# Two edge groups per step with a transposed second layer, and a gather that is partly replaced by column copies, in a graph-network kernel on one Trainium2 core

## The chip, the cores and the metric

The kernel runs on one core of one Trainium2 chip. The metric is the device time of the whole program in microseconds (us); lower is better. The core has five engines that run their own instruction streams and meet at semaphores: PE (matrix products, with weight loads shown as PEld), ACT (activations, and one queue that issues transfers), DVE (element-wise work), POOL (here it issues the indirect gathers), and SP (it issues transfers). On each engine instructions start in program order.

## The reference, cut to what matters

There are N = 12,500 nodes with 64 features and E = 200,000 edges, sorted by `dst`.

```python
nodes = x[edges].reshape(E, 128)               # x[src] beside x[dst]
ssp = lambda v: softplus(v) - log(2)
gates = ssp(edge_state @ We1 + be1) @ We2 + be2
gates = gates * (1 - sigmoid(5.0 * (dist - 3.5)))
h = ssp(nodes @ Wn1 + bn1) @ Wn2 + bn2         # Wn1 128x128, Wn2 128x64
sums = zeros_like(x).at[dst].add(h * gates)
new = x + ssp(sums @ Ws1 + bs1) @ Ws2 + bs2
out = layernorm(x + new)
```

All of it is float32.

## The kernel before

**Tiling.** Edges are cut into 391 groups of 512 (four slots of 128 edges each, called k = 0 to 3). A group's edge features `eT` stand feature-major, two halves of 256 edges stacked on 128 partitions. Its `x[src]` rows are gathered edge-major into a tile `xg` (128 edges on the partitions, 4 slots of 64 features); `x[dst]` is not gathered: `dst` is sorted, so a window of W = 42 nodes covers a half group, a precomputed `table` holds x @ Wn1's lower half plus bias for each node, and a one-hot matrix of 42 columns (line 293, DVE) selects from that window. The one-hot columns lie behind the 64 features in `xg`.

**One step** (loop of lines 632 to 678, one group ahead in layer 1, `i+1`, and one behind in layer 2, `i`):

- SP issues the loads of group `i+5` (lines 273 to 288) and 7 single-row transfers (256 B each, lines 249 to 263); POOL issues up to four gathers of group `i+14` (line 231).
- PE transposes the four slots of `i+1` (lines 304 and 307), ACT copies the result `xT` out of PSUM (line 314), and ACT issues 9 single-row transfers in three portions of three, after this copy, after the exponential and after the logarithm. The rows so fetched by SP and ACT fill some slots (47 of them) which POOL then does not gather. Row addresses come from eight register loads at a time (line 245).
- PE runs the bias and edge products of layer 1 (lines 319 and 324), the bias of layer 2 (354), the scatter product of group `i-2` (383) and, when `xT` is there, the node product of layer 1 (330).
- ACT takes the exponential (341) and the logarithm (344) of 768 columns; DVE forms the softplus `s` (349).
- PE runs layer 2 of group `i`: two products for the gates (361) and four for the hidden part (366). Here `s` is the stationary operand (a new weight load for each) and `We2` or `Wn2` moves 128 or 64 columns, so that the result `gh` is edge-major. DVE multiplies by the cutoff (375) and forms the message (379). The scatter product multiplies messages by the one-hot columns, and DVE adds the result to `sums` at a window whose place is read into registers (lines 391 and 400).

When enough groups are through, a block of nodes is finished in small parts placed into the following steps (`node_block`, lines 402 to 483). The order on each engine is written by hand (`tc.manual_schedule`); waits for buffers come from the tile pools: `xg` has AHEAD + BEHIND = 19 buffers, `z`, `gh` and `tx` in PSUM two each.

A float32 product is recorded as two matmul instructions with two weight loads; a transpose as one.

Of the kernel before, what the change touches and what calls it, by code (L numbers as in the profile page):

```python
# [69 lines left out]
PREPARE = 5  # L70
BEHIND = 5
CLOSE = 12

# [5 lines left out]
READY = (5, 7)  # L79
LANDED = 4  # L80
CUTOFF = 5.0
EPS = 1e-5
# [22 lines left out]
def slots_by_rows(NG):  # L105

    slots = []
    for queue in range(2):
        n = 0
        for g in range(READY[queue], NG - 2):  # L110
            if (g - READY[queue] - ROWS_FROM + 1) * ROWS[queue] >= (n + 1) * P:
                slots.append((queue, g, K - 1 - queue))
                n += 1
    return slots


# [7 lines left out]
def gnn_resnorm_kernel(ctx: ExitStack, tc: tile.TileContext, a: dict, out: bass.AP, E: int):  # L124
# [55 lines left out]
    eps = const.tile([P, 1], F32, name="eps")  # L180
    ones3 = const.tile([PIECES, HE], BF16, name="ones3")
    be3 = const.tile([PIECES, 2, D], BF16, name="be3")
    row3 = const.tile([PIECES, 2, K, D], BF16, name="row3")
    rs3 = const.tile([PIECES, K, D], BF16, name="rs3")
    wns = const.tile([DW, REST, 2, 2 * D], F32, name="wns")

    xgs, xrs, eTs = {}, {}, {}
    made = {}
# [32 lines left out]
    def gather(g):  # L221

        xg = loads.tile([P, K, P], F32, name="xg", bufs=AHEAD + BEHIND)
        xgs[g] = xg
        for k in range(K):
            if (g, k) in by_rows:
                continue
            if padding(g, k):
                nc.vector.memset(xg[:, k, :D], 0.0)
                continue  # L230
            note(("gather", g), nc.gpsimd.indirect_dma_start(  # L231
                out=xg[:, k, :D], out_offset=None, in_=x,
                in_offset=bass.IndirectOffsetOnAxis(ap=src_i[:, g, k : k + 1], axis=0)))
# [39 lines left out]
    def load(g):  # L273
        old = ("scatter", g - LOADS - 4)
        if g % 2 == 0:
# [3 lines left out]
            for j in range(n):  # L279
                eTs[g + j] = both[:, j]  # L280
            _, at = nc.values_load_multi_w_load_instructions(
                base_i[32:33, 2 * g : 2 * g + 4], engines=[SP], min_val=0, max_val=8 * D * (N - 1),
                skip_runtime_bounds_check_because="they were clamped to these bounds")
            bases[g], bases[g + 1] = at[:2], at[2:]
        for h in range(2):
            behind(note(("load", g), nc.sync.dma_start(
                wns[D:DW, g % REST, h, :].bitcast(U8),
                table_bytes[:, bass.ds(bases[g][h], 8 * D * W)].rearrange("o (w f) -> (o w) f", w=W))), old)

    xTs, zs, us, ss, ghs, hs, msgs, scs = ({} for _ in range(8))  # L290
# [26 lines left out]
    def layer1_bias(g, *needs):  # L317
        zs[g] = z_tile()
        first = nc.tensor.matmul(zs[g][:, 0, :HE], be3.rearrange("q h d -> q (h d)"), ones3, start=True, stop=False,  # L319
                                 skip_group_check=True)  # L320
        behind(first, *needs)

    def layer1_edge(g):
        nc.tensor.matmul(zs[g][:, 0, :HE], we1.rearrange("a h d -> a (h d)"), eTs[g], start=False, stop=True,  # L324
                         skip_group_check=True)

    def layer1_node(g):
        for h in range(2):
            zn = zs[g][:, h, HE * (1 - h) : HE * (2 - h)]
            nc.tensor.matmul(zn, wns[:, g % REST, h, :], xTs[g][:, h], start=True, stop=True,  # L330
                             skip_group_check=True)

# [5 lines left out]
    def exps(g, part=every):  # L338
        if part.start == 0:
            us[g] = work.tile([P, 3 * HE], F32, name="u")  # L340
        nc.scalar.activation(us[g][:, part], z_of(g)[:, part], AF.Exp)  # L341
# [4 lines left out]
    def softplus(g, part=every):  # L346
        if part.start == 0:
            ss[g] = work.tile([P, 3, 2, P], F32, name="s", bufs=3)
        nc.vector.scalar_tensor_tensor(ss[g].rearrange("p i t e -> p (i t e)")[:, part], us[g][:, part], BIG,  # L349
# [27 lines left out]
    def message(g):  # L377
        msgs[g] = work.tile([P, K, D], F32, name="msg", bufs=3)
        nc.vector.tensor_mul(msgs[g], ghs[g][:, 0], hs[g])  # L379
# [15 lines left out]
    def window(g):  # L395
        if g not in window_at:
            window_bases(g)
        for h in range(2):
            part = sums[h * D : (h + 1) * D, bass.ds(window_at[g][h], W)]
            nc.vector.tensor_add(part, part, scs[g][h * D : (h + 1) * D, h * W : (h + 1) * W])  # L400

    def node_block(first, n, pool):
# [87 lines left out]
    with tc.manual_schedule():  # L490
# [4 lines left out]
        with tc.tile_pool(name="prep", bufs=1) as prep:  # L495
# [11 lines left out]
            for i in range(3):  # L507
                load_x(i)
            nc.sync.dma_start(rows_i, a["rows"])
            dist = cut.rearrange("p g k -> p (g k)")  # L510
            nc.sync.dma_start(dist, a["dist_l"])
# [3 lines left out]
            for g in range(AHEAD):  # L515
# [13 lines left out]
            nc.scalar.dma_start(wns[:D].rearrange("f r h o -> f (r h) o"),  # L529
                                a["Wn1"][:D, :].rearrange("f (r o) -> f r o", r=1).to_broadcast([D, 2 * REST, 2 * D]))  # L530

            dst_f = dst_h.bitcast(F32)
# [45 lines left out]
            nc.scalar.dma_start(row_d.rearrange("(o q) f -> o q f", o=1), pieces)  # L578
            rows = prep.tile([PIECES, 4, D], BF16, name="rows")
            nc.scalar.dma_start(rows.rearrange("q i d -> q (i d)"), row_d)  # L580
            for i in range(3, PARTS):
# [4 lines left out]
            for i in range(PARTS):  # L586
# [10 lines left out]
                if i == 1:  # L597
                    nc.vector.tensor_copy(base_i[:1], base_b[:1])
                    nc.vector.tensor_scalar(base_i[32:33], base_b[32:33], float(8 * D), None, OP.mult)
                    nc.vector.tensor_scalar(rows_i, rows_i, float(4 * D), None, OP.mult)  # L600
                    for k in range(2):
                        nc.vector.tensor_copy(be3[:, k, :], rows[:, 0, :])
                    for k in range(K):
                        nc.vector.tensor_copy(row3[:, :, k, :], rows[:, 1:3, :])
# [9 lines left out]

        with tc.tile_pool(name="finish", bufs=1) as finish:
            blocks = list(zip(node_blocks(N), block_steps(N, NG)))
            last = NG - 1
            parts, begun, complete, rest = {}, None, 0, []

# [3 lines left out]

            def behind_by(i):
                close = last - CLOSE
                return [g for g in ([i - 2] if i <= close else []) + ([i - 1] if i >= close else []) if g >= 0]

            for g in range(LOADS - 1):
                load(g)
            for g in range(2):  # L630
                onehot(g)
            for i in range(-1, last - 1):
                now = parts.pop(i, [])
                early = [part for part in now if part.tensor]
                at(load, i + LOADS)
                read_rows(i, 0, ROWS[0])
                fetch(i, 0, ROWS[0])
                if i >= 0:
                    at(gather, i + AHEAD)
                transposes(i + 1, ("load", i + 1), ("gather", i + 1), ("onehot", i + 1))  # L640
                xcopy(i + 1)
                read_rows(i, 1, ROWS[1])
                fetch(i, 1, ROWS[1] - 6)
                layer1_bias(i + 1)
                at(layer2_bias, i)
                for n, g in enumerate(behind_by(i)):
                    scatter(g, zs[i + 1][:, 1, HE + 2 * n * W : HE + 2 * (n + 1) * W])
                layer1_edge(i + 1)
                layer1_node(i + 1)
                exps(i + 1)  # L650
                fetch(i, 1, 3)
                logs(i + 1)
                fetch(i, 1, 3)
                for g in behind_by(i):
                    window(g)
                at(layer2, i)
                for part in early:
                    part.tensor(tx_tile())
                at(hcut, i)
                at(message, i)  # L660
                softplus(i + 1)
                for part in early:
                    part.others()
                at(onehot, i + 3)
                for part in now:
                    if not part.tensor:
                        part.others()
                complete = i
                if blocks and complete >= blocks[0][1] - PREPARE and not begun:
                    begun = node_block(*blocks[0][0], finish)  # L670
                    begun.pop(0).others()
                if blocks and complete >= blocks[0][1]:
                    steps = next(steps for steps in BLOCK_STEPS if i + steps[-1] < last - 1)
# [3 lines left out]
                    blocks.pop(0)  # L677
                    begun = None
            assert len(blocks) == 1 and begun and not parts

# [44 lines left out]
    with tc.If(far > 0), tc.tile_pool(name="outside", bufs=1) as o:  # L725
# [7 lines left out]
        with tc.For_i(0, NG, 1) as g:  # L733
# [20 lines left out]
            for k in range(K):  # L754
# [3 lines left out]
            z = z_tile()  # L758
            nc.tensor.matmul(z[:, 1, :HE], be3.rearrange("q h d -> q (h d)"), ones3, start=True, stop=False,
                             skip_group_check=True)  # L760
# [39 lines left out]
def layouts(inputs):  # L800
# [22 lines left out]
    for queue, columns in enumerate(row_columns(NG)):  # L823
        chosen = [out["src_l"].reshape(P, NG, K)[:, g, k] for q, g, k in slots_by_rows(NG) if q == queue]
        v = padded(np.concatenate(chosen), P * columns, 0).reshape(-1, P, READ)
        rows.append(v.transpose(1, 0, 2).reshape(P, columns))
    out["rows"] = np.ascontiguousarray(np.concatenate(rows, axis=1))
    out["dst_l"] = lanes(dst, dst[-1])
    out["dist_l"] = lanes(dist, 1e6)
# [43 lines left out]
```

## Time and profile before

| what | value |
|---|---|
| median of 3 runs (lowest, highest) | 2687.81 us (2668.61, 2691.71) |
| the profiled execution: time, span | 2686.47 us, 2684.7 us |
| mean granted clock of PE | 0.815 |
| first and last `xT` copy start at | 143.3 us, 2660.5 us of the span |
| PE busy, weight loads busy | 2243.6 us (84%), 1754.9 us (65%) |
| DVE, ACT, POOL busy | 1052.4, 969.6, 1441.8 us (39%, 36%, 54%) |
| gathers by POOL | 1516, 951 ns each |
| single-row transfers issued by ACT, by SP | 3328, 2688 |

In the profile a line such as `L330 PE MATMUL z<-xT,wns ... x1564 | 574.1, 503 | 322.9 <-ACT xT L314 309.5` is read so: source line and engine, operation, written tile and read tiles with shapes, number of instructions, then busy us in total and mean ns of one, then how long the engine stood idle just before these and what ended most of that idle time. `ACTq`, `SPq` and `DVEq` are the sequencers' own instructions: transfers issued and registers loaded. Ends of matmuls are modelled by the profiler. The work between 143.3 and 2660.5 us is 390 steps of the loop, so one step takes 6.45 us on average.

### The profile page before, as it was taken

The page shows a single profiled execution, that of the slowest core. Times are in us where ns is not written, and L with a number is a line of the kernel's source. Part 1 is how long each engine was busy: PE and PEld are TensorE (multiplying, and loading weights), DVE is VectorE, ACT ScalarE, POOL GpSimd, SP SyncE. Part 2 cuts the span into 40 slices and gives each one's busy share as a digit, 9 for nine tenths or more (in the row PEclk, how much of TensorE's full clock was granted, in tenths as well). Part 3 has the DMA queues.
Part 4 walks back from the last instruction along what each step waited for, and adds up shares of the span by engine and source line. Part 5 has one row for each costly group of instructions (what it writes and reads, how often), then busy time and mean ns, then how long its engine had stood idle before and what let it go on. Part 6 is the DMA issues. An engine that isn't in the chain of part 4 may idle for free.

```text
span 2684.7 us, 47845 instructions
## 1 busy us (share of the span) xinstructions
PE 2243.6 (84%) x11373; PEld 1754.9 (65%) x11373; DVE 1052.4 (39%) x2767; ACT 969.6 (36%) x1318; POOL 1441.8 (54%) x1520
## 2 busy tenths in 40 slices
PE   2489888988888888888889788888888888888897
PEld 1467666766666666666667666666666667666676
DVE  1233333333334333344333443434433443444445
ACT  0133333333333333333333333333334333333344
POOL 7335555555555555555555555555555555555520
PEclk9987788788788778788777888778878887787878
DMA  6222222222222212222222222222222222222210
GB/s 159 82 64 52 48 51 49 48 49 48 49 52 50 49 47 51 51 52 47 52 46 50 51 49 53 53 50 53 51 50 50 50 58 48 54 52 50 52 44 25
DMA packets 150911, 143.53 MB, mean 53 GB/s; under 512 B 51887, under 2 KB 98395, under 8 KB 150626
## 3 DMA queue, kind: packets, MB, share of 16 engines
q1 hardware_dynamic: 94090, 88.26, 11.6%
q0 software_dynamic: 48512, 49.77, 9.5%
q10 hardware_dynamic: 8024, 2.37, 0.4%
q8 instruction: 97, 1.59, 0.2%
q14 instruction: 188, 1.54, 0.2%
HBM read 130.59 MB, written 9.63 MB: 52 GB/s over the span
## 4 chain that ended last, share of the span: by engine, by line
PE 64%; another core or an unknown queue 11%; ACTq 10%; ACT 7%; issue 5%; DVE 1%; DMA 0%; DVEq 0%; SPq 0%
PE z L330 16%; PE gh L366 12%; PE z L383 10%; ACTq L257 10%; PE gh L361 7%; PE tx L307 6%; ACT xT L314 6%; PE z L324 4%; PE gh L354 3%; PE z L319 2%; PE tx L419 1%; PE z L591 1%; ACTq L245 1%; PE tx L450 1%
## 5 line engine op out<-in xcount | busy, mean ns | idle before, releaser
L231 POOL DMA_INDIRECT xg<-in_x,src_i x1516 | 1441.6, 951 | 1144.8 <-PE z L383 353.1
L330 PE MATMUL z<-xT,wns 106*128 106x256 f32 x1564 | 574.1, 503 | 322.9 <-ACT xT L314 309.5
L330 PEld LDWEIGHTS z<-xT,wns 106*128 106x128 f32 x1564 | 361.3, 246 | 486.6 <-ACT xT L314 407.9
L341 ACT ACTIVATE u<-z 128x768 f32<-128x768 f32 x392 | 317.4, 810 | 830.4 <-issue 362.4
L366 PE MATMUL gh<-consts,s 128*128 128x64 f32 x3128 | 493.1, 313 | 0.0
L400 DVE TENSOR_TENSOR sums<-sums,z 64x42 f32 x778 | 153.0, 197 | 863.4 <-issue 626.8
L366 PEld LDWEIGHTS gh<-consts,s 128*128 128x128 f32 x3128 | 490.2, 238 | 0.1
L314 ACT COPY xT<-tx 106x512 f32<-106x512 f32 x391 | 228.9, 586 | 670.9 <-remote 231.5
L375 DVE TENSOR_TENSOR h<-gh,cut 128x256 f32<-128x256 f32 x391 | 166.1, 425 | 618.2 <-PE z L383 239.7
L344 ACT ACTIVATE u<-u,one 128x768 f32<-128x768 f32 x392 | 365.9, 934 | 69.7 <-issue 53.3
L349 DVE SCALAR_TENSOR_TENSOR s<-u,z 128x768 f32<-128x768 f32 x392 | 369.4, 943 | 11.1 <-ACT u L344 9.8
L361 PEld LDWEIGHTS gh<-consts,s 128*128 128x128 f32 x1564 | 304.0, 247 | 70.1 <-DVE s L349 32.8
L383 PEld LDWEIGHTS z<-xg,msg 128*128 128x128 f32 x1556 | 240.3, 221 | 152.8 <-issue 148.5
L361 PE MATMUL gh<-consts,s 128*128 128x128 f32 x1564 | 313.8, 335 | 1.8 <-DVE s L349 1.8
L383 PE MATMUL z<-xg,msg 128*128 128x84 f32 x1556 | 306.2, 327 | 0.9 <-DVE msg L379 0.2
L324 PE MATMUL z<-eT,consts 128*128 128x256 f32 x782 | 295.4, 465 | 0.0
L307 PE MATMUL tx<-consts,xg 128*106 128x128 f32 x1517 | 278.6, 312 | 6.4 <-DMA wns<-table 6.4
L307 PEld LDWEIGHTS tx<-consts,xg 128*106 128x106 f32 x1517 | 216.0, 169 | 10.6 <-issue 8.0
L379 DVE TENSOR_TENSOR msg<-gh,h 128x256 f32<-128x256 f32 x391 | 166.0, 425 | 13.4
L354 PE MATMUL gh<-row,ones 3*128 3x512 bf16 x391 | 170.0, 435 | 0.0
L324 PEld LDWEIGHTS z<-eT,consts 128*128 128x128 f32 x782 | 141.7, 226 | 1.2 <-issue 1.2
L293 DVE TENSOR_TENSOR xg<-consts,rel 128x168 f32<-128x168 f32 x391 | 129.9, 332 | 0.0
(93 smaller groups left out, 609.5 us busy)
## 6 DMA issues: line engine op xcount, KB each, us to landing
xr<-in_x ACTq DMA_DIRECT2D x3328, 0.2 KB
eT<-in_eT SPq DMA_DIRECT2D x195, 256.0 KB
xr<-in_x SPq DMA_DIRECT2D x2688, 0.2 KB
xg<-in_x,src_i POOLq DMA_INDIRECT x1516
wns<-table SPq DMA_DIRECT2D x782, 21.0 KB
table<-tb SPq DMA_DIRECT2D x14, 448.0 KB
sums<-in_xT SPq DMA_DIRECT2D x7, 455.0 KB
y<-in_x SPq DMA_DIRECT2D x24, 128.0 KB
```

The source lines that it names most:

```text
L231: note(("gather", g), nc.gpsimd.indirect_dma_start(out=xg[:, k, :D], out_offset=None, in_=x, in_offset=bass.IndirectOffsetOnAxis(ap=src_i[ ...
L257: ins = queues[queue].dma_start(row_tiles[n, "in"][r : r + 1, :D].bitcast(U8), x_bytes[:, bass.ds(row_at[queue].pop(0), 4 * D)])
L307: ins = nc.tensor.transpose(tx[:, k, :], xgs[g][:, k, :DW], ident)
L314: note(("xcopy", g), nc.scalar.copy(xT, xTs[g]))
L324: nc.tensor.matmul(zs[g][:, 0, :HE], we1.rearrange("a h d -> a (h d)"), eTs[g], start=False, stop=True, skip_group_check=True)
L330: nc.tensor.matmul(zn, wns[:, g % REST, h, :], xTs[g][:, h], start=True, stop=True, skip_group_check=True)
L341: nc.scalar.activation(us[g][:, part], z_of(g)[:, part], AF.Exp)
L344: nc.scalar.activation(us[g][:, part], us[g][:, part], AF.Ln, bias=one)
L349: nc.vector.scalar_tensor_tensor(ss[g].rearrange("p i t e -> p (i t e)")[:, part], us[g][:, part], BIG, z_of(g)[:, part], OP.min, OP.max)
L361: nc.tensor.matmul(v[:, 0, t], ss[g][:, 0, t, :], we2, start=False, stop=False, skip_group_check=True)
L366: nc.tensor.matmul(ghs[g][:, 1, 2 * t + h, :], ss[g][:, 1 + h, t, :], wn2, start=False, stop=h == 1 and t == 1, skip_group_check=True)
L383: ins = nc.tensor.matmul(sc, msgs[g][:, 2 * t : 2 * t + 2, :].rearrange("p h f -> p (h f)"), xgs[g][:, 2 * t : 2 * t + 2, D:DW], start=t = ...
```

## The change

Groups 0 to 371 are now worked in 186 pairs, one pair per step (`PAIRS = 186`); the last groups keep the old step. In a pair's step:

- Layer 1's bias and edge products run once for both groups with 512 moving columns (`pair_edge`); the node products stay one set per group. The exponential, logarithm and softplus are done in two parts: 1024 columns (edges of both groups and nodes of the first) and 512 columns (nodes of the second).
- Layer 2 is feature-major: `We2` and `Wn2` are stationary and `s` moves 512 columns. `pair_gates` is one product; `pair_hidden` is two, each with the 64 columns of `Wn2` as weights, writing partitions 0 to 63 and 64 to 127 of one bank. ACT adds the gates' bias while it copies them out of PSUM (`pair_bias`, 128x512), DVE adds the hidden part's bias and multiplies (`pair_products`, 128x512), PE transposes the product back to edge-major (`pair_turn`, four transposes of 128x128), and DVE applies the cutoff (`pair_weigh`, 128x512). Scatter and windows of a pair come a step later.
- The step's gathers, one-hots, loads and single-row transfers are those of two groups: 14 rows by SP, 18 by ACT in six portions of three. ACT's logarithm of the first part is followed at once by the second group's `xT` copy.
- x is loaded once, transposed and in two halves stacked on the partitions, into an SBUF tile `xh` of 6250 columns. From group 8 on DVE copies 16 columns of it a pair (two calls of `columns`, each eight register loads and eight copies of one 128x1 column at a register's place) into a tile of 128 columns, the `x[src]` of one slot. When a tile is full, a mask keeps the half that holds the wanted node, and one extra product per such slot adds `wn1_twice` times that tile to the node product (`node_half`). In all 23 slots come from 2944 such copies; POOL's gathers fall from 1516 to 1493. For these slots DVE clears the 64 feature columns of `xg` instead.
- `xg` has 20 buffers instead of 19; the loads of SP wait for a scatter that is four groups further back.

On DVE the built order within a step is: `pair_weigh` of the pair before, two one-hots, the 16 column copies, `pair_products`, the softplus of 1024 columns, the window adds of the pair before (register load and four adds), the softplus of 512 columns. On PE it is: transposes of the first group, layer 1 bias and edge, `pair_gates`, node products of the first group, transposes of the second, `pair_hidden`, scatter of the pair before, `pair_turn`, node products of the second.

```diff
-BEHIND = 5
-CLOSE = 12
+BEHIND = 6
+PAIRS = 186
+COLUMNS = 8
+COLUMNS_FROM = 8
+XH_PARTS = 4
...
+def slots_by_columns(NG):
+
+    slots = []
+    for g in range(NG - 2):
+        if (g - 5 - COLUMNS_FROM + 1) * COLUMNS >= (len(slots) + 1) * P:
+            slots.append((g, 1))
+    return slots
...
-        old = ("scatter", g - LOADS - 4)
+        old = ("scatter", g - LOADS - 8)
...
+    def columns(i, pool):
+
+        n = columns_done[0]
+        if i < COLUMNS_FROM or n >= len(by_columns) * P:
+            return
+        p, q = (n // COLUMNS) % P, n // (COLUMNS * P) * COLUMNS
+        _, at = nc.values_load_multi_w_load_instructions(
+            columns_i[p : p + 1, q : q + COLUMNS], engines=[DVE], min_val=0, max_val=half_n - 1,
+            skip_runtime_bounds_check_because="src holds rows of x")
...
+        for j in range(COLUMNS):
+            nc.vector.tensor_copy(column_tiles[slot][:, n % P + j : n % P + j + 1], xh[:, bass.ds(at[j], 1)])
...
+    def pair_gates(p):
+        gates2[p] = gh_tile()
+        nc.tensor.matmul(gates2[p], we2.rearrange("a h d -> a (h d)"), s2s[p][:, :NB], start=True, stop=True,
+                         skip_group_check=True)
+
+    def pair_hidden(p):
+        hidden2[p] = gh_tile()
+        nodes = s2s[p][:, NB:].rearrange("p (j h e) -> p h j e", j=2, h=2)
+        for h in range(2):
+            nc.tensor.matmul(hidden2[p][h * D : (h + 1) * D].rearrange("p (j e) -> p j e", j=2), wn2, nodes[:, h],
+                             start=True, stop=True, skip_group_check=True)
+
+    def pair_bias(p):
+        turned2[p] = work.tile([P, NB], F32, name="mT")
+        nc.scalar.activation(turned2[p], gates2[p], AF.Identity, bias=sides2[:, 0:1])
+
+    def pair_products(p):
+        nc.vector.scalar_tensor_tensor(turned2[p], hidden2[p], sides2[:, 1:2], turned2[p], OP.add, OP.mult)
+
+    def pair_turn(p):
+        for t in range(K):
+            part = slice(t * P, (t + 1) * P)
+            nc.tensor.transpose(hidden2[p][:, part], turned2[p][:, part], ident)
...
+            for p in range(-1, PAIRS):
+                i, m, single = 2 * p, 2 * p + 2, p == PAIRS - 1
...
+                transposes(m, ("load", m), ("gather", m), ("onehot", m))
+                xcopy(m)
+                read_rows(i, 1, ROWS[1])
+                fetch(i, 1, 3)
...
+                    pair_edge(p + 1)
+                if p >= 0:
+                    pair_gates(p)
+                    pair_bias(p)
+                if p >= 1:
+                    pair_weigh(p - 1)
+                fetch(i, 1, 3)
...
+                    pair_node(p + 1, 0)
+                    pair_exps(p + 1, 0)
+                fetch(i, 1, 3)
+                transposes(m + 1, ("load", m + 1), ("gather", m + 1), ("onehot", m + 1))
+                for j in range(2):
+                    at(onehot, i + 4 + j)
+                for j in range(2):
+                    columns(i + j, finish)
+                if p >= 0:
+                    pair_hidden(p)
...
+                if p >= 0:
+                    pair_products(p)
...
+                    pair_logs(p + 1, 0)
+                    xcopy(m + 1)
+                    z2s[p + 1] = z_tile()
+                read_rows(i + 1, 1, ROWS[1])
+                fetch(i + 1, 1, 3)
+                if p >= 1:
+                    pair_scatter(p - 1, zs[m + 1][:, 1, HE:] if single else z2s[p + 1][:, 0])
+                if p >= 0:
+                    pair_turn(p)
...
+                    pair_node(p + 1, 1)
+                    pair_exps(p + 1, 1)
+                    fetch(i + 1, 1, 3)
+                    pair_logs(p + 1, 1)
+                    pair_softplus(p + 1, 0)
+                fetch(i + 1, 1, 3)
...
+                if p >= 1:
+                    pair_windows(p - 1)
...
+                    pair_softplus(p + 1, 1)
```

## The prediction, made before the changed kernel ran

> **What bounds the kernel now.** I read the page's engine table and slices first, then the chain, then the timeline and the chain in order of time around 1300 us. The page:
>
> ```profile
> PE 2243.6 (84%) x11373; PEld 1754.9 (65%) x11373; DVE 1052.4 (39%) x2767; ACT 969.6 (36%) x1318; POOL 1441.8 (54%) x1520
> PEclk9987788788788778788777888778878887787878
> PE 64%; another core or an unknown queue 11%; ACTq 10%; ACT 7%; issue 5%; DVE 1%; DMA 0%; DVEq 0%; SPq 0%
> L349 DVE SCALAR_TENSOR_TENSOR s<-u,z 128x768 f32<-128x768 f32 x392 | 369.4, 943 | 11.1 <-ACT u L344 9.8
> ```
>
> No engine is full, and PE's clock is seven to eight tenths all the way. The timeline of one step:
>
> ```profile
> 1301.13 0.60 PE L307 MATMUL tx<-consts,xg 128*106 128x128 f32 x4
> 1301.99 0.81 ACT L341 ACTIVATE u<-z 128x768 f32<-128x768 f32 x1 [3.17 <-PE tx L307]
> 1302.06 0.85 ACTq L257 DMA_DIRECT2D xr<-in_x  x3
> 1302.96 0.93 ACT L344 ACTIVATE u<-u,one 128x768 f32<-128x768 f32 x1 [0.16 <-ACT u L341]
> 1303.40 0.95 POOL L231 DMA_INDIRECT xg<-in_x,src_i  x1 [0.30 <-issue]
> 1304.65 0.94 POOL L231 DMA_INDIRECT xg<-in_x,src_i  x1 [0.30 <-issue]
> 1305.09 0.59 ACT L314 COPY xT<-tx 106x512 f32<-106x512 f32 x1 [0.61 <-remote]
> 1305.94 1.08 ACTq L257 DMA_DIRECT2D xr<-in_x  x3
> ```
>
> The transposes (L307) end at 1301.73 by the model, yet the copy that waits for them starts at 1305.09. Over 330 middle steps the copy starts a median 1.65 us (95%: 3.1) after its last transpose, while the exponential starts a median 0.19 after its last node product. So a transpose's release comes late, and the step is a ring: copy, node product, layer 2, transposes, late release, copy. The chain in order of time gives PE's share at both clocks:
>
> ```profile
> 1300.00 0.45 PE gh L361 x4
> 1300.45 0.84 PE gh L366 x8
> 1301.29 0.44 PE tx L307 x4
> 1303.23 2.50 issue
> 1305.72 1.13 PE z L330 x4
> 1306.86 0.74 PE gh L361 x4
> 1307.60 1.60 PE gh L366 x8
> 1309.20 0.85 PE tx L307 x4
> 1312.80 2.00 PE z L330 x4
> ```
>
> From 1300.00 to 1303.23 plus L330 PE needs 4.36 us a step; from 1306.86 to 1314.80, at half the clock, 7.94. After the 2.5 us gap the clock halved. In the clock records it is either full or half, in stretches of 3.41 us; the last stretch before a fall has PE busy 0.33 to 0.65 of it (5% to 95%), stretches before that 0.66 to 1. So a late release costs twice: the gap, and then a slow stretch. Mean step: 6.45 us, or 12.9 a pair.
>
> **The change, part by part, per pair, full clock unless said.**
>
> *PE.* Before: 2 x 4.36 = 8.7. After: transposes 2 x 0.44, bias 0.22, edge 0.94 (L324's pair of 256 columns takes 0.47), gates 0.94 at the same rate, node products 2 x 1.13, hidden 0.94 (if the two halves of the array work side by side) to 1.88 (one after the other), scatter 2 x 0.60, turn 0.44: 7.8 to 8.8. PE gains nothing as work. What moves is the order: the transposes of one group now stand right behind the node products of the other, with 2 to 3 us of ACT work before their copies are due. This takes the late release out of the ring for the most part.
>
> *ACT with its queue.* A copy with its register load and three transfers takes 1.93 (1305.09 to 1307.02), an activation with three transfers 0.97 (1301.99 to 1302.96). New: the Identity of 128x512, about 0.59 as the copy; it hides under its three transfers, and if they went it would cost that 0.59. Exponential of 1024 columns: 0.811 at 768 and 0.577 at 512 make 1.05; logarithm 0.935 and 0.721 make 1.15. Sum: 1.93 + 0.97 + 1.10 + 1.20 + 1.93 + 0.97 + 0.97 = 9.1, against 2 x 3.9 before its waits.
>
> *POOL.* 1493/391 x 2 = 7.64 gathers at a pitch of 1.25 (1303.40 to 1304.65): 9.55. The 23 slots are 29 us of POOL in all, 0.15 a pair; POOL waited before, so this alone is worth nothing.
>
> *SP* keeps its 14 row transfers; the `xh` parts (four transfers of 0.8 MB) and 23 side rows go past them early and rarely: 3 us at the start, hidden later by loads that run steps ahead. The 20th `xg` buffer and the loads' older scatter only loosen waits that were over anyway. Each of the 23 slots also takes a mask, a product and a clear on DVE (at most 0.33 each, as the one-hot of 168 columns) and one matmul: about 1 us x 23, 0.12 a pair, beside other work.
>
> *DVE* is where the change adds. Removed: two h and two msg products of 0.425 = 1.70. Added: `pair_products` 0.68 and `pair_weigh` 0.69 (0.425 at 256 columns, plus 0.26 for 256 more by L349's 680 ns at 512 and 943 at 768). Then the columns: two loads of eight registers and 16 copies. Their rows:
>
> ```profile
> L245 ACTq TENSOR_LOAD <-rows_i x416: 548/728/886, 143.3 to 2542.7; - x139
> L391 DVEq TENSOR_LOAD <-base_i x391: 522/528/810, 158.1 to 2665.3; - x196
> 110.39 0.18 DVE L604 COPY row<-rows 3x128 bf16<-3x128 bf16 x1
> 110.49 0.16 DVE L605 COPY rs<-rows 3x64 bf16<-3x64 bf16 x1
> ```
>
> Loads: 0.73 each as on ACT, 0.33 of the first under a one-hot: 1.13. A copy: the small copies at 110 us start 0.095 apart, a floor, since they set no address; the window adds (L400), which set one, start 0.204 apart, a ceiling, since they also read PSUM. I take 0.135, nearer to the copies as the operation is a copy: 16 make 2.2 (1.5 to 3.3).
>
> The copies stand before `pair_products`, and behind that wait `pair_turn`, the second node products, the second exponential and logarithm, the second softplus, and the next step's weigh and columns: a ring. Its sum: products 0.68, turn 0.60, node 1.13, release 0.19, exponential to logarithm 0.97, logarithm of 512 0.72, softplus of 512 0.68, weigh 0.69, one-hots 2 x 0.33, loads 1.13, copies 2.2 = 9.65 (8.95 to 10.75). Node-block work on DVE (about 103 us in all) puts 0.3 into it. Half clock on turn and node adds 1.1 to 1.7 us; for a quarter of the time, 0.3. That is 10.25, above ACT's 9.1 and POOL's 9.55. The hidden product's late release is under the columns for about 0.9, the transposes' under 1.5 to 2; what sticks out of medians of 1.4 to 1.65 with a tail of 3 I put at 0.75 (estimate). **11.0 a pair.**
>
> *Sum.* 143 to the first copy and 3 of added loads, 187 x 11.0 = 2057, 17 old steps x 6.45 = 110, 24 from the last copy to the end: 2337, plus 1.8 outside the span: 2339, so **2340 us** against the profiled 2686.5, which lies 1.3 below the median of the runs.
>
> *Two rules weighed.* DVE copies beside POOL's gathers: 25 of the 47 xr copies (L296, 128x42) lie wholly inside a gather and take their 0.186 as elsewhere; those gathers took 0.997 on average against a median of 0.947, so 0.05 a copy, 0.8 a pair, POOL 10.35, still inside the 11.0. The Trainium skill (SBUF — State Buffer, "two separate sides") says that a float32 SBUF-to-SBUF copy on DVE locks POOL out of writing descriptors until about 115 ns after it ends. By that, with 0.16 a copy, 16 copies would cost POOL 4.4 a pair: 13.95, and 2890 us in all. The clock: this trace halves it after stretches merely half idle. The skill (TensorE: Matmul & The Clock Gate, Part 1) asks for a whole idle window of 3.4 us; by that the 0.3 would go, and the sum be 2284.
>
> **The rivals.**
> A. *POOL bounds.* Copies at the floor and releases covered leave 9.55 plus a little, 9.7: 2100 us. For it: POOL's pitch never fell below 1.25. Against: DVE's ring is longer in the middle of its bounds.
> B. *Late releases stay.* The second node products' release turns as late as a transpose's (1.65 instead of 0.19), since PE no longer pauses behind them, and the clock stays half for 0.37 of the time instead of a quarter: 11.0 + 1.46 + 0.17 = 12.6: 2640 us at its full price. For it: the share of PE work is as before.
> C. *Slower: the columns.* 12.85 a pair is where nothing is won, so a copy's pitch of 0.135 + 1.85/16 = 0.25 decides. At 0.30 it is 13.6: 2830 us. For it: no row shows a DVE copy from a register's address, with a register set between any two. Against: the window adds do the same at 0.204.
> D. *It doesn't do what it says:* turn and hidden put two more hand-overs into PE's order, and the pair stays at twice the old step, 12.9: 2700 us.
>
> **How the numbers follow.** The forecast's own case (10 to 11.8 a pair, 2150 to 2490) has 0.50, A 0.10, B (from 2490 to its full price) 0.22, C 0.13, D 0.05. A measurement of this kernel tells about 1% from no change, 27 us. Faster (below 2660): 0.50 + 0.10 + 0.20 of B = 0.80; the same: 0.04 of D and 0.02 of B = 0.06; slower: C and the rest of D, 0.14. The range leaves out C and D: 2100 to 2640.
>
> **What would show it.** Right: `xT` copies two per 11 us, seldom waiting over 1 us for transposes; DVE's 16 copies in 2 to 2.5 us; `pair_products` starting right behind the last copy and PE's turn right behind that; clock above 0.85; gathers near 0.95. Wrong: copies over 0.25 apart (C), gathers over 1.1 (the lock), turn waiting for the hidden release and not for the columns (B), POOL without gaps (A).

## The result, and the profile after

The changed kernel took 3086.95 us (median of 4, 3084.9 to 3092.94), the kernel before 2682.27 beside it (median of 4, 2668.61 to 2691.71): ratio 1.1517, 95% interval 1.1459 to 1.1575. The prediction was 2340, with 2640 as its upper end: wrong in size and in sign. One plain fact is needed to read all that follows: the first batch of experiments met the same times for the kernel before (2665 to 2695), but five later batches, on five other chips, measured that same kernel at 1935 to 1941 us. Ratios are therefore taken only within a batch, and the two settings are called the 2680 chip and the 1937 chips. The names are for short: no chip was met twice, and which chip took the times of this section is not on record, so that the chip itself makes the difference is likely but not shown.

The profiled execution of the changed kernel has a span of 3083.8 us and a mean clock of 0.774 (before: 2684.7 and 0.815). A pair takes 15.2 us, measured from one `pair_products` to the next. The page of the changed kernel:

```profile
PE 2057.9 (67%) x7887; PEld 1221.0 (40%) x7887; DVE 1334.6 (43%) x5417; ACT 1072.9 (35%) x1504; POOL 1420.6 (46%) x1497
...
PEclk9987777777777777777786778777777777777778
...
SPq 13%; PE 12%; issue 10%; DMA 5%; DVE 2%; ACTq 2%; ACT 1%; DVEq 1%; another core or an unknown queue 0%
...
L255 POOL DMA_INDIRECT xg<-in_x,src_i x1493 | 1420.4, 951 | 1564.7 <-DVE mT L504 561.5
...
L357 PE MATMUL tx<-consts,xg 128*106 128x128 f32 x1517 | 290.2, 320 | 399.2 <-DMA wns<-table 232.7
...
L332 DVE COPY column<-xh 128x1 f32 x2944 | 314.7, 150 | 314.2 <-issue 311.0
...
L354 PE MATMUL tx<-consts,xr 128*106 128x128 f32 x47 | 18.3, 389 | 200.4 <-DMA xr<-in_x 200.4
```

No engine but DVE is busier than before in its share. The chain, which was 64% PE, is now led by `SPq`, the queue of SP that was 0% of it; but it could be followed over the last 46% of the span only. The transposes wait for the table rows `wns` (232.7 us) and for the row slots `xr` (200.4 us). In the page of the kernel before the first of these waits was small, and the second was not there:

```profile
L307 PE MATMUL tx<-consts,xg 128*106 128x128 f32 x1517 | 278.6, 312 | 6.4 <-DMA wns<-table 6.4
```

The 200.4 us can be put down to one queue. SP fills 21 of the 47 row slots and ACT 26, and they stand at different places of a group: PE waits before 20 of SP's 21, a median 10.4 us each, and before none of ACT's. And the table loads, which were issued a median 37 us before the `xT` copy of their group in the kernel before, are issued 8 us before it now (from 500 to 2400 us). The gathers are as long as ever. Does SP itself wait for anybody? In the answer for SP's waits in the changed kernel (engine and line, what it waited for, us in all, times, longest), the largest rows of the middle are:

```profile
SPq L311 <- PE z L379: 9.4, 23, 1.1
SPq L311 <- DMA wns<-table: 8.0, 7, 1.4
```

So it hardly does: its waits from 500 to 2400 us add up to some 34 us, against 97 in the kernel before, where SP ran so far ahead that it waited for the scatter that frees its buffers:

```profile
SPq L278 <- PE z L383: 85.0, 78, 4.4
```

SP issues almost without a pause and is late all the same. SP's timeline over one pair of the changed kernel (start, us, then what was issued) shows the order of the round, one `eT`, four table loads, 14 rows:

```profile
1495.41 0.36 SPq L302 DMA_DIRECT2D eT<-in_eT  x1
1496.47 1.80 SPq L311 DMA_DIRECT2D wns<-table  x4
1499.23 12.42 SPq L281 DMA_DIRECT2D xr<-in_x  x14
1511.70 0.36 SPq L302 DMA_DIRECT2D eT<-in_eT  x1
```

The round is 16.3 us here. Summed from 500 to 2400 us, by the time from each of SP's instructions to its next, a pair is 7.8 for 14 rows, 2.0 for register loads, 4.7 for four table loads and 0.5 for `eT`: 15.0 of the 15.2. In the kernel before the same sum was 7.85, 2.05, 2.05 and 0.4: 12.4 of 13.1. The 2.7 us more are all in the table loads, 0.51 each before and 1.18 now: of the 1500 rows that SP has for them in this stretch (a check of a semaphore, a register move and an issue for each load) 290 took 0.6 us or more, and so did 288 of the gaps that follow them; in the kernel before it was 8 and 22 of 1309. What lengthens them can be seen on DVE at the same time, in its timeline (in brackets the idle time before, and what ended it):

```profile
1504.76 0.57 DVE L332 COPY column<-xh 128x1 f32 x8
1505.66 0.39 DVE L332 COPY column<-xh 128x1 f32 x3 [0.34 <-issue]
...
1507.77 0.15 DVE L332 COPY column<-xh 128x1 f32 x1 [0.57 <-issue]
1508.52 0.15 DVE L332 COPY column<-xh 128x1 f32 x1 [0.59 <-issue]
```

Eight copies run in 0.57 us, and then single ones stand 0.73 apart. In such stretches, the trace's rows of register moves and of the issues of row transfers take about 0.7 us instead of 0.03 to 0.25, on SP, DVE and ACT alike. These are called stalls here: from 500 to 2400 us, 435 of SP's, 190 of DVE's and 210 of ACT's, 484 us together where overlaps are counted once (before: 405 of SP's, none of DVE's, one of ACT's; 300 us).

Single rows in these stretches can't be trusted to the microsecond. The packets of SP's row transfers, which the DMA engines record themselves, start 0.85 to 1.5 us after the row that issues them in run 9 below; here 14% of them start before it, by up to 2.0 us, so the rows are recorded late. The sums hold: from the first to the last packet of a pair's 14 rows it takes 8.1 us on average here and 5.2 in run 9. The list of waits is incomplete too: this trace has 20,074 semaphore events and run 9 has 57,268, with as many instructions and DMA packets.

### The profile page after: what moved, and what is told of

Read it like the earlier page. It is cut to its first block, busy times and chain, and to the rows that moved or that the text cites. A ratio compares the mean times of both kernels' runs of the same rounds, so it can differ in the third digit from the quotient of the medians.

```text
span 3083.8 us, 47159 instructions
## 1 busy us (share of the span) xinstructions
PE 2057.9 (67%) x7887; PEld 1221.0 (40%) x7887; DVE 1334.6 (43%) x5417; ACT 1072.9 (35%) x1504; POOL 1420.6 (46%) x1497
## 5 line engine op out<-in xcount | busy, mean ns | idle before, releaser
L357 PE MATMUL tx<-consts,xg 128*106 128x128 f32 x1517 | 290.2, 320 | 399.2 <-DMA wns<-table 232.7
L476 ACT ACTIVATE u<-z 128x1024 f32<-128x1024 f32 x372 | 301.6, 811 | 552.8 <-PE z L379 238.1
L504 DVE SCALAR_TENSOR_TENSOR mT<-gh,sides,mT 128x512 f32<-128x512 f32 x186 | 139.6, 751 | 790.7 <-PE gh L496 674.8
L332 DVE COPY column<-xh 128x1 f32 x2944 | 314.7, 150 | 314.2 <-issue 311.0
L484 DVE SCALAR_TENSOR_TENSOR s<-u,z 128x1024 f32<-128x1024 f32 x372 | 355.0, 954 | 212.0 <-issue 117.4
L479 ACT ACTIVATE u<-u,one 128x1024 f32<-128x1024 f32 x372 | 347.8, 935 | 86.2 <-issue 56.1
L501 ACT ACTIVATE mT<-gh,sides 128x512 f32<-128x512 f32 x186 | 127.8, 687 | 639.8 <-PE gh L489 230.5
L463 PE MATMUL z<-eT,consts 128*128 128x512 f32 x372 | 334.2, 996 | 0.0
L489 PE MATMUL gh<-s,consts 128*128 128x512 f32 x372 | 282.0, 852 | 0.0
L509 PE MATMUL gh<-consts,mT 128*128 128x128 f32 x744 | 135.1, 310 | 182.8 <-DVE mT L504 161.5
L496 PE MATMUL gh<-s,consts 128*64 128x512 f32 x744 | 210.5, 645 | 0.0
L354 PE MATMUL tx<-consts,xr 128*106 128x128 f32 x47 | 18.3, 389 | 200.4 <-DMA xr<-in_x 200.4
```

What stands on the lines that cost most here:

```text
L332: nc.vector.tensor_copy(column_tiles[slot][:, n % P + j : n % P + j + 1], xh[:, bass.ds(at[j], 1)])
L357: ins = nc.tensor.transpose(tx[:, k, :], xgs[g][:, k, :DW], ident)
L463: nc.tensor.matmul(z1s[p][:, 0], we1.rearrange("a h d -> a (h d)"), eT2s[p], start=False, stop=True, skip_group_check=True)
L476: nc.scalar.activation(u2s[p, j], pair_z(p, j), AF.Exp)
L479: nc.scalar.activation(u2s[p, j], u2s[p, j], AF.Ln, bias=one)
L484: nc.vector.scalar_tensor_tensor(s2s[p][:, slice(4 * HE, 6 * HE) if j else slice(0, 4 * HE)], u2s[p, j], BIG, pair_z(p, j), OP.min, OP.max)
```

## The experiments

Theory SP: SP's in-order queue of row transfers and table loads bounds the changed kernel. Its rivals: the columns' copies on DVE do; or late releases of PE's semaphores do, whatever the queues hold. Each ratio is to the kernel before in the same batch. The diffs show the lines that matter; where rows are taken away, two more lines only let a list be empty.

**First batch, the 2680 chip (before: 2678.32).**

1. *Pairs without columns.*

```diff
-XH_PARTS = 4
+XH_PARTS = 0
...
-    by_columns = {slot: n for n, slot in enumerate(slots_by_columns(NG))}
+    by_columns = {}
```

> Leaves out the columns' whole share: no copies, no xh, and the 23 slots keep cleared rows instead of source rows (1493 gathers as after). Theory SP (the sync queue is the bound: in the changed kernel's middle it issues without a pause, about 15 us a pair, of which 14 row transfers with their register moves are 7.7, four table loads 4.7 and register loads 2): SP loses only the stalls that the copies' register moves share with it, so 13 to 14.5 us a pair, 2700 to 3000 us. Theory columns (the 16 copies, 3.3 us a pair with a mean pitch of 0.209, hold back products, turn and the second half of the pair): 15.0 less 3.3, 11.7 a pair, 2470 us or less.

3079.62 us, 1.1506 (1.1439 to 1.1573). One correction: with no slot set aside, POOL gathers the 23 slots too (1516), here and in the next kernels without columns, so nothing is left out. The copies cost nothing that can be measured; the pair stays at 15.1 us. The columns theory, and with it rival C of the prediction, falls.

2. *Pairs without SP's rows.*

```diff
-ROWS = (7, 9)
+ROWS = (0, 9)
```

> SP fetches no rows; POOL gathers those 21 slots instead (1514). Theory SP: SP's pair falls from 15 to some 6 us, so the transposes no longer wait for table loads (232.7 us) or row slots (200.4 us); the next ring, POOL at 7.74 x 1.25 = 9.7 or DVE at 10 to 12, sets the pair: 2150 to 2550 us. Theory columns: little changes, 2950 to 3090 us.

2614.11 us, 0.9754 (0.9695 to 0.9812): 466 us less than run 1 of the same batch, with all the columns. That is what theory SP asks for, and the table loads are issued 40 us ahead again; the time itself lies above its 2150 to 2550. The page says what is next:

```profile
PE 32%; ACTq 25%; issue 19%; ACT 14%; another core or an unknown queue 4%; DVE 4%; DMA 1%; DVEq 1%; SPq 0%
ACTq L281 23%; PE z L379 11%; ACT u L479 5%; PE z L463 5%; PE gh L489 3%; PE tx L357 3%; ACT u L476 3%; PE gh L496 2%; ACT xT L364 2%; PE z L438 2%; ACTq L269 2%; ACT mT L501 2%; PE z L461 1%; PE z L725 1%
```

SP is out of the chain and ACT's queue is in, with its 18 rows a pair (L281). They took some 0.47 each, 8.5 us of a pair of 12.6, and 406 of ACT's moves and issues stalled. That ACT's queue bounds this kernel was not tested by an edit.

3. *Neither columns nor SP's rows* (both edits above).

> Without the columns (their 23 slots keep cleared rows instead of source rows) and without SP's rows (POOL gathers 1514). Theory SP: as without SP's rows alone or up to 200 us under it, 2100 to 2400. Theory columns: as without the columns alone. If both stand at 12 us a pair or more, late releases of PE's semaphores hold the pair whatever the queues do.

2621.23 us, 0.9782 (0.9724 to 0.9839): as the one before, so the columns are hidden here too.

4. *The kernel before without SP's rows* (the edit of run 2).

> The kernel before without SP's rows (POOL gathers 1537). Theory SP: SP waited for almost nothing in the kernel before either (119 us for the scatters in all), so its 6.45 us a step were SP's as much as PE's; without 3.9 us of row transfers a step it loses at least the steps that waited for SP: 2450 to 2620 us. If late releases alone set the step before: 2660 to 2700. POOL's gathers need 3.93 x 1.25 = 4.9 a step, so POOL does not bound it.

2623.63 us, 0.983 (0.9754 to 0.9905): 2% for a queue that was 95% full, just above the range. The late release is still there: the copy of the transposes starts a median 1.59 us after them, though no register move or row issue stalls any more. Late releases thus do not need the stalls; that they are all the rest is not shown.

**Second batch, a 1937 chip (before: 1940.72).** The clock is 0.96 to 0.99. No register move takes over 0.1 us and no row's issue over 0.6; of SP's larger transfers a few (3 to 26 of over 900) take 0.5 to 1.7.

5. *Pairs without any rows.*

```diff
-ROWS = (7, 9)
+ROWS = (0, 0)
```

> Neither SP nor ACT fetches rows; POOL gathers all slots but the columns' (1540, 7.88 a pair). Theory queues (an in-order queue that issues row transfers bounds the pair: SP at 15 us, and once SP was free ACT, whose queue holds 25% of the chain at 12.3 us a pair): both are free, and POOL at 7.88 x 1.25 = 9.8 us or DVE at 9.7 to 11 sets the pair: 2000 to 2250 us. Theory releases (late releases of PE's semaphores hold the pair at 12.3 whatever the queues do): 2550 to 2650.

1975.6 us, 1.0183 (1.0164 to 1.0201); again on another chip (no_rows_second) 1973.62, 1.019 (1.0167 to 1.0213).

6. *The kernel before without any rows* (the same edit).

> The kernel before without any row transfer; POOL gathers 1563 slots, 4.0 a step, 5.0 us. Theory queues: ACT's transfers between copy, exponential and logarithm go, PE's 4.36 us and ACT's 2.4 us with POOL's 5.0 remain: 2150 to 2450 us. Theory releases: transposes' releases still come 1.6 us late, which keeps the ring of copy, node product, layer 2 and transposes at about 6.2 us: 2550 to 2640.

1997.3 us, 1.0292 (1.0274 to 1.0309). The copies start a median 0.04 us after the transposes.

7. *Pairs without rows or columns* (the edits of 1 and 5; 1563 gathers).

> No rows and no columns (their 23 slots keep cleared rows instead of source rows; POOL gathers 1540). With the queues out of the way this prices the columns where nothing hides them: if DVE's ring bounds the pair without rows, 2.2 to 3.3 us a pair less than with the columns, 400 to 600 us; if POOL or PE does, the same time within 1%.

2003.0 us, 1.0321 (1.0304 to 1.0339). The columns are worth 27 us here, POOL's time for 23 gathers, and cost nothing.

These three show what bounds them on a 1937 chip: gathers at a pitch of 1.25 us, from one start to the next, with hardly a gap (five or six pauses, 4 us in all). The last gather ends 28 to 34 us before the kernel does. 1540 x 1.25 and 50 make 1975, 1563 x 1.25 and 43 to 49 make 1997 to 2003, and the kernel before is 1516 x 1.25 and 41 to 46. They do not tell theory SP from the rival as meant, since the setting had changed. And they warn of a label: in run 5 the page has 234.7 us of transposes waiting for `wns<-table`, as much as the changed kernel's 232.7, with the table loads issued 32 us ahead and POOL as the bound:

```profile
L357 PE MATMUL tx<-consts,xg 128*106 128x128 f32 x1564 | 242.1, 277 | 300.9 <-DMA wns<-table 234.7
```

The wait by that name alone does not speak against SP; the row slots and the 8 us do.

8. *The changed kernel without gathers.*

```diff
-            note(("gather", g), nc.gpsimd.indirect_dma_start(
-                out=xg[:, k, :D], out_offset=None, in_=x,
-                in_offset=bass.IndirectOffsetOnAxis(ap=src_i[:, g, k : k + 1], axis=0)))
+            note(("gather", g), nc.gpsimd.memset(xg[:, k, :D], 1.0))
```

> The changed kernel with POOL clearing the 1493 slots to ones instead of gathering them, so those edges get no source rows; rows by SP and ACT and the columns stay. In the changed kernel the register moves and issues of SP, ACT and DVE take 0.70 to 0.73 us instead of 0.03 to 0.25 in stretches, 484 of 1900 us. If the gathers in flight cause them, they vanish and the pair falls to 12 us or less: under 2450 us. If the row transfers of SP and ACT cause them among themselves, they stay and so does SP's 15 us a pair: 2950 to 3090.

1949.16 us, 1.0054 (1.0038 to 1.007); on three more 1937 chips 1952.25, 1956.79 and 1953.02 (the last two one run each). The slots are set to ones, so it leaves out what the gathers bring. It was meant for the stalls, and says nothing of them where there are none. What it does say comes with the next run.

**Third batch, a 1937 chip (before: 1936.61).**

9. *The changed kernel itself,* with no edit.

> The changed kernel itself, next to the kernel before. On the chip of the second batch the kernel before took 1941 us with PE's clock at 0.97 and no register move or issue over 0.5 us; on that of the first 2680 with the clock at 0.82 and stalls of 0.70 to 0.73. Theory SP with stalls: where the kernel before takes about 2680, 3080 again; where it takes about 1941, SP's pair needs 14 x 0.33 + 4 x 0.45 + 2.3 + 0.5, some 9.2 us, ACT's 9.1 and POOL's 9.55: 1940 to 2050 us, within 5% of the kernel before. Theory that the pairs' own order costs the 15%: 1.15 of the kernel before on either, so 2230 where it takes 1941.

1956.16 us, 1.0111 (1.009 to 1.0132). The 15% does not belong to the order of the pairs alone. Its page:

```profile
PEclk9999999999999999999999999999999999989998
...
PE 26%; ACTq 23%; ACT 19%; issue 12%; DVE 9%; DMA 4%; SPq 3%; DVEq 2%; POOL 2%; POOLq 0%
...
L255 POOL DMA_INDIRECT xg<-in_x,src_i x1493 | 1418.2, 950 | 458.8 <-issue 340.9
...
L332 DVE COPY column<-xh 128x1 f32 x2944 | 303.6, 150 | 134.4 <-issue 133.7
L357 PE MATMUL tx<-consts,xg 128*106 128x128 f32 x1517 | 237.4, 276 | 8.7 <-DMA wns<-table 8.7
```

The wait for table rows is 8.7 us instead of 232.7, and PE waits over 1 us before 6 of SP's 21 row slots instead of 20. With 1493 gathers POOL would end near 1866 and 47, 1913; the last gather ends 73 us before the kernel does, not 28 to 34, and the kernel takes 1956 with the gathers and 1949 to 1957 without them, so here POOL does not hold it, and the queues are the likely bound. Which of the two it is was not told apart: the chain names ACT and its queue (42% together), but SP's round is as full, as its timeline shows against the 16.3 us above:

```profile
1001.74 0.36 SPq L302 DMA_DIRECT2D eT<-in_eT  x1
1002.81 1.79 SPq L311 DMA_DIRECT2D wns<-table  x4
1005.54 5.40 SPq L281 DMA_DIRECT2D xr<-in_x  x14
1010.99 0.36 SPq L302 DMA_DIRECT2D eT<-in_eT  x1
```

14 rows take 5.40 us, not 12.42; the sum a pair is 9.3 of 9.47.

**Fourth to sixth batch, 1937 chips.**

10. *Three rows a step on SP and three on ACT.*

```diff
-ROWS = (7, 9)
+ROWS = (3, 3)
-                fetch(i, 1, 3)
+                fetch(i, 1, ROWS[1] // 3)
```

The same is done at ACT's other `fetch` calls.

> The changed kernel with 3 rows a step on SP and 3 on ACT instead of 7 and 9; POOL gathers 1523 slots, the columns stay. Theory queues: where the kernel before takes about 2680, SP's pair of 15 us loses 8 rows at 0.55 and ACT's of 12.3 loses 12 rows at 0.46, so neither is over 10.6 and POOL's 9.7 or DVE's 10 to 11 sets the pair: 2050 to 2350 us, under both kernels. Where the kernel before takes about 1940, POOL's pitch of 1.25 us bounds every version without a full ACT queue: 1523 x 1.25 and 45 to 50 at the ends, 1950. Theory releases: 2550 or more where the kernel before takes 2680, since late releases do not depend on the number of rows.

1949.31 us, 1.0076 (1.006 to 1.0093): POOL's line for 1523 gathers, as written for this setting.

11. *Nine rows on SP, six on ACT* (the edit of run 10 with `ROWS = (9, 6)`).

> The changed kernel with 9 rows a step on SP and 6 on ACT instead of 7 and 9 (1496 gathers). Where the kernel before takes about 2680, theory SP: four more rows a pair at 0.55 with their share of the stalls, 15.0 and 2.2 to 3.3: 17.2 to 18.3 a pair, 3500 to 3700 us. Theory that ACT's queue or the releases hold the pair: 3080 or less. Where the kernel before takes about 1937, POOL bounds the kernel before (1516 gathers at a pitch of 1.25 and 42 us) and ACT's full queue the changed one; here ACT has 7.1 us a pair, SP 9.0 or less, POOL 9.55: 1496 x 1.25 and 45 to 50, 1915 to 1925 us, 0.6 to 1.1% under the kernel before.

2263.22 us, 1.1687 (1.1667 to 1.1706), where 1915 to 1925 was expected. SP's sum had been put at 9.0 or less; it is 18 rows at 0.33, 2.25 register loads at 0.83 and one at 0.57, four table loads at 0.51 and `eT` at 0.44: 10.9, and the pair takes 11.1. A round of SP, and then the page:

```profile
1004.42 0.56 SPq L302 DMA_DIRECT2D eT<-in_eT  x1
1005.68 1.85 SPq L311 DMA_DIRECT2D wns<-table  x4
1008.51 7.25 SPq L281 DMA_DIRECT2D xr<-in_x  x18
1015.81 0.37 SPq L302 DMA_DIRECT2D eT<-in_eT  x1
```

```profile
PE 52%; SPq 19%; DMA 9%; issue 8%; DVE 7%; ACT 2%; DVEq 2%; ACTq 1%; POOL 1%; POOLq 0%
...
L357 PE MATMUL tx<-consts,xg 128*106 128x128 f32 x1520 | 251.5, 288 | 203.1 <-DMA wns<-table 182.0
```

That is the picture of the 2680 chip again: the queue of SP is in the chain, PE waits over 1 us before 26 of SP's 27 row slots and before none of ACT's 17, and the table loads are issued a median 9 us ahead. But no register move of SP or DVE takes over 0.1 us and no row's issue of SP over 0.5, and ACT has fewer rows. So a full queue of SP costs this much without any stall. The clock falls with it, to 0.87.

12. *Six and six* (`ROWS = (6, 6)`).

> The changed kernel with 6 rows a step on SP and 6 on ACT (1505 gathers). Where the kernel before takes about 1937: SP's pair measured 10.97 us with 9 rows a step, so 12 rows and 1.5 register loads leave 8.4; ACT's is 7.1; POOL's 7.70 x 1.25 = 9.6 bounds: 1505 x 1.25 and 45 to 50, 1925 to 1932 us, 0.3 to 0.6% under the kernel before. Where it takes about 2680: SP's 15 us less 2 rows at 0.55 and a share of the stalls, 13 to 13.9 a pair: 2700 to 2880 us.

1929.68 us, 0.9961 (0.9947 to 0.9974), as expected. With both queues slack (the table loads are issued 29 us ahead) the pairs beat the kernel before by 0.4%, and the changed kernel, which stood at 1.0111 of it on another chip, by some 1.5%: POOL's line for 1505 gathers.

```profile
L255 POOL DMA_INDIRECT xg<-in_x,src_i x1505 | 1430.6, 951 | 461.5 <-issue 320.6
```

13. *The kernel before itself, with no edit, and without gathers* (the edit of run 8: its 1516 slots are set to ones by POOL).

> The kernel before itself, for its profile where it takes about 1937 us: 1516 gathers at a gapless pitch of 1.25 and 42 us at the ends would make 1937, so POOL should show no idle time but the 0.30 between gathers, the copies of the transposes should start within 0.3 us of the last transpose instead of a median 1.65, and PE's clock be over 0.95.

> The kernel before with POOL clearing its 1516 slots to ones instead of gathering them (those edges get no source rows). Where the kernel before takes about 1937: if POOL alone bounds it, this is faster, down to SP's 4.6 us a step or PE's 4.4: 1850 to 1930. Where it takes about 2680: if gathers in flight make PE's releases late and SP stall, 1850 to 2100; if not, 2550 to 2700.

1937.37 and 1899.17 us (one run each). In the page of the kernel before, on a 1937 chip:

```profile
PEclk9999999999999999999999999999999999999998
...
L231 POOL DMA_INDIRECT xg<-in_x,src_i x1516 | 1442.4, 951 | 465.3 <-issue 359.6
```

465.3 us idle over 1516 gathers is 0.31 each, the gap within the pitch: POOL hardly waits, and its last gather ends 27 us before the kernel does. The copies start a median of 0.1 to 0.25 us, by the stretch taken, after the transposes instead of 1.65. Without gathers the kernel before is 1899 and the changed one 1949 to 1957: where POOL does not hide it, the pair order with full queues is the slower of the two.

**Two expectations of repeated runs,** no_gathers_again (1952.25 us) and no_gathers_fourth (1953.02 us):

> The changed kernel with POOL clearing the 1493 slots to ones instead of gathering them (those edges get no source rows). Where the kernel before takes about 2680: if gathers in flight cause the stalls of SP, ACT and DVE, they vanish and this takes under 2450 us; if the row transfers cause them among themselves, 2950 to 3090. Where the kernel before takes about 1941 it took 1949 and showed no stall.

> The changed kernel with POOL clearing the 1493 slots to ones instead of gathering them (those edges get no source rows). Where the kernel before takes about 2680: under 2450 us and no stall of 0.7 us if gathers in flight cause the stalls; 2950 to 3090 with stalls if the row transfers cause them among themselves or something outside the kernel does. Where the kernel before takes about 1937, 1950 again.

## Why the prediction was wrong, step by step

- **The step that failed: SP.** The prediction says that SP "keeps its 14 row transfers" and puts no time on them, nor on the table loads and register loads; only the added `xh` parts and side rows have a price, "3 us at the start, hidden later by loads that run steps ahead". So SP's round never stood beside ACT's 9.1, POOL's 9.55 and DVE's 10.25; it was taken as hidden without a reason. It was 12.4 of 13.1 us in the kernel before, to be had from its own trace by adding the rows of its instructions. In a pair's time of 12.9 it was hidden, with loads 37 us ahead; in the 11.0 of the forecast it could not be, and with 12.4 in place of 11.0 the same sum gives 2600 us. It then became 15.0, which is nearly the whole pair: of the 4.2 us that the forecast's pair lacks, 1.4 could have been read ahead and 2.7 is the growth, which no view showed, as stalls that had fallen on SP's row transfers now fell on its table loads too (where nothing stalls the round is 9.3, run 9). Without SP's rows the changed kernel loses some 470 us (run 2); with more of them it is 16% longer also where nothing stalls (run 11 against run 9).
- **The columns** were put at 2.2 us with bounds 1.5 to 3.3. With the second register load between the two eights counted in, they took 3.3 on the 2680 chip (mean pitch 0.21) and 2.2 on a 1937 chip (0.14); inside an eight the pitch was 0.17 and 0.10, so the 0.135 was too long without stalls and too short with them, within its bounds of 0.095 and 0.204. Taking them out gained nothing in either setting (runs 1, 3 and 7). Rival C was right in the sign by luck: its reason was wrong.
- **ACT's queue at 9.1, POOL at 9.55 a pair:** POOL's is right: its pitch was 1.25 everywhere, and rival A, POOL as the bound, is what every 1937 chip shows as soon as the queues are slack (runs 5 to 7, 10, 12). ACT's 9.1 was not measured by itself; the pair of run 9, 9.47, leaves room for it. On the 2680 chip, with SP out of the way, ACT's queue leads the chain of a pair of 12.6.
- **The late release as PE's main loss** was a true reading of the profile shown and not a property of the order: the same kernel has at most 0.25 us instead of 1.65 elsewhere. Rival B, that the releases stay, described run 2 (2614 us against its 2640), but with ACT's queue beside it, so the two are not told apart there.
- **The clock** was to be above 0.85; it was 0.774. With SP's rows gone it was 0.829, and 0.975 in run 9, so it goes with PE's waits; a clock cause of its own was not tested.
- **The two rules weighed.** 2944 copies from SBUF to SBUF left the gathers at 951 and 950 ns and their pitch at 1.25: the rule of the Trainium skill (SBUF — State Buffer, "two separate sides") that such a copy locks POOL out does not show here, for copies of a single column. The rule on the clock was not tested by itself.

**Open:** what makes moves and issues stall on the 2680 chip, and whether it is the chip or something else that went with that batch. The same kernel with the same gathers and rows shows no stall elsewhere (run 9), so these alone do not make them; on that chip they vanish from the kernel before when SP's rows go (run 4), but move to ACT in the pairs (run 2). Whether gathers in flight take part was not seen, since the kernel without gathers never met that chip.

## What to carry to other kernels

Add up each issuing queue's round, register loads and moves included, before calling a transfer hidden: a queue that waits for nobody is a bound, and one that is 95% full is a bound for any step that is to become shorter, even where the chain gives it 0%. See how far ahead its transfers are issued, for a wait may bear the name of a transfer that landed long ago. A row transfer of 256 B cost SP 0.33 us at best, 42 us for the 128 that save POOL one gather of 1.25, so such rows pay only in a queue with room to spare. And ask what in a profile could belong to the chip or the hour: the kernel before took 1.38 times as long in one batch as in five others on other chips.

## What the runs showed of the hardware

- The same program took 2680 us on one chip and 1937 on five, with TensorE's mean clock at 0.82 and 0.98.
- In the slow setting moves and issues of three engines took about 0.7 us in common stretches, and a seventh of SP's row transfers show their packet before the row that issues them, by up to 2.0 us.
- The two halves of the hidden product (512 columns, 64 output rows each) took 1.08 us together at full clock, against 1.02 for the one full product of the gates: they run side by side.
